# Local attention and whitening on one core: ScalarE's kept copies given out inside the halves of sums, some steps of the order moved, and one batch of writes issued from SyncE

## The chip, the cores and the metric

One core of a Trainium2 chip. The metric is the device time of one execution in microseconds (us); times stated for a kernel are the median of several executions. Engines are called PE (TensorE: matmuls and transposes; PEld is its weight load), DVE (VectorE), ACT (ScalarE), POOL (GpSimd) and SP (SyncE). SP, ACT and POOL also issue DMAs.

## What is computed

The input x has shape (4, 256, 64, 64), all in float32. Two layers follow one another; cut to what matters:

```python
# layer 0
k = conv(x, w1, 7x7, dilation 2, padding 6) + b1      # 256 -> 128 channels
k = conv(k, w2, 1x1) + b2                             # 128 -> 49
attn = softmax(k, axis=1)                             # one weight for each of 49 taps
shifts = stack([xp[:, :, 2*u:2*u+64, 2*v:2*v+64] for u in range(7) for v in range(7)])
y = einsum('bkchw,bkhw->bchw', shifts, attn)          # weighted sum of 49 shifted inputs
# layer 1, for each of 4 groups of 64 channels over all images
Sigma = eps*I + xc @ xc.T / m                         # xc: y less its mean
P = five Newton steps towards Sigma**(-1/2)
out = (P @ xc) * weight + bias
```

## The kernel before

**Convolution.** The two convolutions are merged into one with 49 outputs. By the dilation, each image falls into parities of rows and columns, and the 7x7 convolution is done on them as a transformed one (points of evaluation along rows, `ROWS` 0 to 5 and `INF`, and along columns, grouped in three `BANKS`). One step is `conv_step(k, i)` (line 828): the matmuls of one bank into a PSUM tile `cv` (L603) and their eviction by ACT into `pv` (L614, L619), in `conv_bank` (line 577); then `prepare` (line 819) makes the operands for the same bank of the next row: `weights` (DVE, and scalings on ACT at L481), `row_eval` (DVE; for row 0 two plain copies rb<-slot on ACT, L510) and `col_eval` (DVE into `xh`, and one plain copy xh<-rb on ACT, L545 or L551). For row 0 of an image `weights` also issues a load from SP, rb<-g0d, of weights kept in DRAM, and DMAs that copy pieces of them. `col_interp` and `row_interp` (DVE) bring results back to logits.

**Kept work of ACT.** The copies and scalings on ACT that `prepare` makes are not traced at once. They are put in the list `points`, and the next `conv_bank` traces them behind its own eviction; a dependency that orders issue only keeps them behind it. The list `later` does the same for the last copies of an interpolation (L710, L737), after bank 1 only.

**Attention.** Each image has four quarters, n = 4b to 4b+3. For a quarter, the softmaxed weights d are copied into a padded tile `zt` (`move_terms`, line 1095: eleven small copies, L1127 on ACT, or L1139 on DVE for the last image), written to a DRAM scratch `sd` by eight DMAs (L1146), and read back skewed as `band` and `bandz` by `load_band` (L1196, L1208, on SP). `weighted_sum` (L1316) then is a matmul of a block of transposed inputs with the band. A quarter is done in two halves:

- `first_half(n)` (line 1452): for each block, `make_blocks` transposes x on PE (L1252) and evicts it on ACT, xb<-tp (L1283) and for edges xbz<-tp (L1274); the sums; `store_y` evicts y in place of x (L1338, ACT). In between stand the turns of the quarter before: `turn_y` transposes y (L1388) and evicts yt<-tp (L1398, ACT); `moments` multiplies yt with itself into `sig` (L1407).
- `second_half(n, mid)` (line 1492): the same for the lower half, with the turns of its own upper half, `make_blocks` of the next quarter's first block, `moments`, and `bands(n + 1, last)`, which loads the next band and moves the terms of the quarter after it.
- `finish()` (line 1444) does the two turns and moments that the next first half would have done; for odd n it calls `move`, which spills a slot of x and y to DRAM (L1431) and loads the next image's x into it (L159), both from POOL.

**Order.** PE runs in the order of the trace, since every matmul is tied to the one before it. Evictions on ACT are marked with a high priority, and a scheduler that runs at compile time fixes each engine's order from priorities, dependencies and its own estimate of times. The main loop runs the convolution of image b and cuts it by cost into eight stretches; at the end of each, `gap(b, j)` runs what `plan` has put there, for instance the halves of sums of image b-1. With the steps' costs, the halves of image 0 stand in gaps (1,2) to (1,7), (2,0) and (2,1), with `finish` behind the fourth; those of image 1 one image later; those of image 2 in gaps (3,3) to (3,7), and its last three and all of image 3's behind the loop, where they are called by hand as `rest[...]`. The step in front of gap (2,0) and of gap (3,0) is `direct_inf`, a direct convolution of one row (L770).

Of the kernel before, what the change touches and what calls it, by code (L numbers as in the profile page):

```python
# [32 lines left out]
def kernel(  # L33
# [29 lines left out]
    nc = tc.nc  # L63
# [508 lines left out]

    slot = {}

    later, points = [], []

    def conv_bank(b, br, i, w):

        if i == 0:
            slot[b, br] = len(slot) % NV if b == 0 else (len(slot) - NV) % 2  # L580
        pts = BANKS[i]
        i0 = sum(len(k) for k in BANKS[:i])
        cv = cv_buf[ncv[0] % 2][:, : 3 * PT].rearrange("p (n q f) -> p n q f", n=3, q=Q9)
        ncv[0] += 1
        if b == 0:
            xv = {bc: xh[bc].rearrange("p (q e f) -> p e q f", e=2 * NCC, q=Q8) for bc in pts}
        else:
            xv = {
                bc: xh[bc].rearrange("p (e g q f) -> p e q g f", e=2 * NCC, g=2, q=Q8)
                for bc in pts  # L590
            }
        for k, bc in enumerate(pts):
            terms = [(sr, sc, cc) for sc in taps(bc) for sr in taps(br) for cc in range(NCC)]
            wv = w[bc].rearrange("p c (a r k) -> p c r a k", r=len(taps(br)), a=NCC)
            for j, (sr, sc, cc) in enumerate(terms):
                for h in range(2):
                    o = cv[
                        h * HB : h * HB + KT, k, sr : sr + Q8, 2 * sc : 2 * (sc + Q8)
                    ]
                    if b > 0:  # L600
                        o = o.rearrange("p q (g f) -> p q g f", g=2)
                    pe(
                        nc.tensor.matmul(  # L603
                            o,
                            wv[:, sc, sr, cc],
                            xv[bc][:, h * NCC + cc],
                            start=(j == 0),
                            stop=(j == len(terms) - 1),
                            skip_group_check=True,
                        )  # L610
                    )
        with tc.high_priority():
            full_ = len(pts) - (INF in pts)
            last = nc.scalar.copy(  # L614
                pv[:K2, slot[b, br], i0 : i0 + full_].rearrange("p n q b -> p (n q b)"),
                cv[:K2, :full_].rearrange("p n q f -> p (n q f)"),
            )
            if INF in pts:
                last = nc.scalar.copy(  # L619
                    pv[:K2, slot[b, br], i0 + full_].rearrange("p q b -> p (q b)").rearrange(  # L620
                        "p (q f) -> p q f", q=Q9
                    )[:, :, : 2 * Q8],
                    cv[:K2, full_, :, : 2 * Q8],
                )
        for waiting in (points, later) if i == 1 else (points,):
            while waiting:
                with tc.high_priority() if waiting is points else nullcontext():
                    copied = waiting.pop()()
                for one in copied if isinstance(copied, list) else [copied]:
                    tc.add_manual_dep(  # L630
                        one.ins,
                        last.ins.name,
                        mybir.DependencyInfo(
                            mybir.DependencyClass.NoSync, mybir.DependencyReason.DATA
                        ),
                        reason="later",
                    )

    def interpolate(pt, tmp, outs, cut, part=None, pairs=None):

# [187 lines left out]
    def conv_step(k, i):  # L828
        w = {bc: nxt.pop(bc) for bc in BANKS[i]}
        b, br = rows[k]  # L830
        conv_bank(b, br, i, w)
        end = b > 0 and br == ROWS[-1]
        if end:

            with in_order():
                if i == len(BANKS) - 2:
                    col_interp(b, br, 0)
                elif i == len(BANKS) - 1:
                    col_interp(b, br, 1)
                    row_interp(b, 1)  # L840
        last = i == len(BANKS) - 1 and br == ROWS[-2]
        if k + 1 < len(rows):
            with tc.high_priority() if last else nullcontext():
                prepare(k + 1, i, points.append)
        if i == len(BANKS) - 1 and not end:
            with in_order() if last else nullcontext():
                col_interp(b, br)
                if last:
                    row_interp(b, 0)
# [245 lines left out]
    def move_terms(n, after=None):  # L1095
# [46 lines left out]
        for g in range(CR):  # L1142
            for h in range(2):
                p0 = g * SW + h * TC
                queue = nc.sync if h and n == 4 * (B - 1) else nc.gpsimd
                dma = queue.dma_start(  # L1146
                    bass.AP(
                        tensor=D.tensor,
                        offset=D.offset + h * HS + g * RS,
                        ap=[[LS, TC], [CR * RS, NCH], [1, KS * WS]],  # L1150
                    ),
                    zt[p0 : p0 + TC, R : R + NCH * KS].rearrange(
                        "p (m e) w -> p m (e w)", e=KS
                    ),
                )
                if queue is nc.gpsimd:
                    written[:] = [dma]
# [283 lines left out]

    half_done = {-1}

    def finish():

        n = open_n.pop()
        for t8 in (2, 3):
            turn_y(n, t8)
        moments(n, 1)
        if n % 2:  # L1450
            move(n // 2)

    def first_half(n):
        last = open_n.pop() if open_n else None

        def turn(t8):
            if last is not None:
                turn_y(last, t8)

        def block(t8):  # L1460
            if (n, (t8, 0)) not in blocks:
                make_blocks(n, t8)

        block(0)
        turn(2)
        weighted_sum(n, 0, 0)
        block(1)
        weighted_sum(n, 0, 1)
        block(2)
        weighted_sum(n, 0, 2)  # L1470
        turn(3)
        weighted_sum(n, 0, 3)
        weighted_sum(n, 0, 4)
        move_terms(n + 1, store_y(n, 0))
        half_done.add(n)
        load_band(n + 1, 0)
        make_blocks(n, 3, y_dve.get((n, 0))) if (n, (3, 0)) not in blocks else None
        if last is not None:
            moments(last, 1)
            if last % 2:  # L1480
                move(last // 2)

    def bands(n, after=None):

# [4 lines left out]
            load_band(n, 1)  # L1489
            move_terms(n + 1, after)  # L1490

    def second_half(n, mid=None):
        turned = turn_y(n, 0)
        if n % 4 == 3:
            bands(n + 1, turned)
        weighted_sum(n, 1, 0)
        weighted_sum(n, 1, 1)
        turn_y(n, 1)
        weighted_sum(n, 1, 2)
        weighted_sum(n, 1, 3)  # L1500
        weighted_sum(n, 1, 4)
        if mid is not None:
            mid()
        last = store_y(n, 1)
        if n + 1 < 4 * B:
            make_blocks(n + 1, 0, y_dve.get((n, 1)))
        moments(n, 0)
        open_n.append(n)
        done.add(n)
        bands(n + 1, last)  # L1510

# [24 lines left out]
    for b in range(B):  # L1536
        hs = [
            (lambda *a, n=n, f=f: f(n, *a))
            for n in range(4 * b, 4 * b + 4)
            for f in (first_half, second_half)  # L1540
        ]
        if b + 2 < B:
            for j in range(8):
                plan(b + 1, 2 + j, hs[j])
                if j == 3:

                    plan(b + 1, 2 + j, finish)
        else:
            for j in range(8):
                if b == B - 1 or 3 + j >= NPC:  # L1550
                    rest.append(hs[j])
                else:
                    plan(b + 1, 3 + j, hs[j])
    for b in range(B - 1):
        for j in range(2) if b else ():
            plan(b + 1, b * j, lambda b=b, j=j: soft(b, j))

    slots[4] = store[4]
    pieces = read_x(halves(store[4]), 4, nc.sync)
    for j in range(2, 6):  # L1560
# [6 lines left out]
    for b in range(1, B):  # L1567
# [12 lines left out]
            steps.insert(0, (12, lambda b=b: direct_inf(b)))  # L1580
        j, at, whole = 0, 0, sum(c for c, _ in steps)
        for cost, f in steps:
            f()
            while rest_of:
                rest_of.pop()()
            at += cost
            if at * NPC >= (j + 1) * whole:
                gap(b, j)
                j += 1
    apool.release()  # L1590
    rpool = ctx.enter_context(tc.tile_pool(name="rp", bufs=1, reuse_waits="tile"))

# [29 lines left out]
    rest[1]()  # L1622
    move_terms(n + 1)
    rest[2]()
    finish()
    soft_start(1, False)
    move_terms(n + 2)
    for t8 in range(4):
        if (n, (t8, 0)) not in blocks:
            make_blocks(n, t8)  # L1630
    rest[3]()
    rest[4]()
    soft_rows(1, 1)
    for f in rest[5:-2]:
# [242 lines left out]
```

## Time and profile before

| what | value |
|---|---|
| times of 3 runs | 680.88, 682.57, 682.58 us; median 682.57 |
| profiled execution | 680.68 us; its span 678.7 us |
| PE busy | 648.2 us (96%) |
| PEld busy | 527.6 us (78%) |
| DVE busy | 566.3 us (83%) |
| ACT busy | 332.7 us (49%) |
| POOL busy | 117.2 us (17%) |
| granted TensorE clock | 0.996 |
| DMA moved | 126.09 MB |
| sd<-zt, POOL, 77 KB | 124 DMAs, 3.3 us from issue to landing in the median |
| spill<-slot, POOL, 2048 KB | 3 DMAs, 10.5 us |

The span runs from the first to the last instruction that the profile shows; the execution's own time has some 2 us around it. A matmul counts as busy from its start to an end that is modelled, so the busy share of PE says little; its idle time and who ended it say more. In a timeline row, the first two numbers are start and length in us, then come engine, line, operation, output<-input and shape, and in brackets the idle time before it and what ended that. The order of first blocks, turns and sums can be followed by line: L1252 transposes x, L1283 evicts it, L1316 sums, L1338 evicts y, L1388 turns it, L1398 evicts it, L1407 takes moments.

The gaps stand in the profile at these times (start of the first PE instruction of the half): gap (1,2) at 189.1, (1,5) with its `finish` at 238.7, (1,6) at 259.5, (2,0) at 289.5, (2,2) at 327.6, (2,5) at 379.6, (3,3) at 477.4. The last convolution ends at 540.8.

### The profile page before, as it was taken

To read this page: it belongs to the slowest core of one execution; us is meant where nothing else is said; L and a number is where in the kernel's file an instruction comes from. 1 tells how busy PE (TensorE), PEld (TensorE's weight loads), DVE (VectorE), ACT (ScalarE), POOL (GpSimd) and SP (SyncE) were. 2 spreads that over 40 slices of the span, in tenths; PEclk is the share of its full clock that TensorE was granted. 3 is DMA by queue.
4 is the path that set the end of the run, shared out by engine and by line. 5 is a ranking of instruction groups with operands and counts; after the bars stand their busy time and mean duration, and the time that the engine had idled before them with its cause. 6 is when DMAs were issued, how large, how long until landed. Compare 5 with 4: busy or idle time off the path is not lost.

```text
span 678.7 us, 19071 instructions
## 1 busy us (share of the span) xinstructions
PE 648.2 (96%) x7800; PEld 527.6 (78%) x7800; DVE 566.3 (83%) x1240; ACT 332.7 (49%) x862; POOL 117.2 (17%) x177
## 2 busy tenths in 40 slices
PE   6999999999999999999899999999999999999993
PEld 1439573357899988889899998999899999998430
DVE  3699999999389889999999589989998987633673
ACT  1424331023565555566755554464854566634663
POOL 0000550662213020001122020002130203400000
PEclk9999999999999999999999999999999999999998
DMA  8961899993599979313587485027374325649698
GB/s 318 248 162 67 138 262 361 217 185 50 116 208 224 228 160 370 120 60 84 166 269 245 139 279 189 2 67 190 94 199 111 71 63 123 166 98 384 237 404 354
DMA packets 110607, 126.09 MB, mean 186 GB/s; under 512 B 69255, under 2 KB 91896, under 8 KB 109368
## 3 DMA queue, kind: packets, MB, share of 16 engines
q1 hardware_dynamic: 93528, 69.03, 35.3%
q0 software_dynamic: 10944, 37.57, 22.1%
q10 hardware_dynamic: 6048, 18.27, 8.8%
q8 instruction: 61, 1.00, 0.6%
q14 instruction: 26, 0.21, 0.1%
HBM read 78.78 MB, written 52.36 MB: 193 GB/s over the span
## 4 chain that ended last, share of the span: by engine, by line
PE 67%; DVE 19%; ACT 6%; DMA 4%; issue 2%; POOL 0%; ACTq 0%; DVEq 0%; SPq 0%; POOLq 0%
PE cv L603 24%; PE y L1316 10%; PE cv L770 8%; PE acc L770 8%; PE sig L1407 4%; PE tp L1388 3%; DMA out_dram<-out 3%; PE tp L1252 2%; DVE pv L352 2%; DVE zz L352 2%; PE cv L251 2%; DVE xh L352 2%; DVE ct L352 2%; DVE zz L348 1%; DVE zz L345 1%
## 5 line engine op out<-in xcount | busy, mean ns | idle before, releaser
L603 PE MATMUL cv<-xh,wr 128*49 128x128 f32 x4160 | 232.6, 273 | 0.2
L603 PEld LDWEIGHTS cv<-xh,wr 128*49 128x49 f32 x4160 | 226.1, 124 | 3.3 <-issue 1.0
L1146 POOL DMA_DIRECT2D sd<-zt x124 | 65.2, 532 | 334.6 <-ACT zt L1127 269.6
L1316 PE MATMUL y<-band,xb 128*128 128x209 f32 x448 | 93.9, 342 | 4.7 <-ACT xb L1283 2.7
L1316 PEld LDWEIGHTS y<-band,xb 128*128 128x128 f32 x448 | 75.7, 190 | 6.0 <-ACT xb L1283 3.3
L614 ACT COPY pv<-cv 113x486 f32<-113x486 f32 (+2 forms) x60 | 26.0, 433 | 90.6 <-PE cv L603 90.3
L352 DVE SCALAR_TENSOR_TENSOR pv<-pv 113x162 f32<-113x162 f32 x176 | 53.1, 322 | 2.2 <-ACT pv L614 1.4
L1127 ACT COPY zt<-d 32x112 f32<-32x112 f32 (+2 forms) x132 | 38.5, 292 | 14.9 <-DVE d L997 9.3
L1398 ACT COPY yt<-tp 128x512 f32<-128x512 f32 x60 | 34.9, 593 | 21.1 <-PE tp L1388 20.5
L1388 PE MATMUL tp<-ident,slot 128*128 128x128 f32 x240 | 41.5, 296 | 1.0 <-ACT slot L1338 1.0
L1049 ACT ACTIVATE d<-tp,mx 128x49 f32<-128x49 f32 x96 | 27.5, 322 | 28.0 <-DVE mx L1046 28.0
L1252 PE MATMUL tp<-ident,slot 128*128 128x128 f32 x256 | 40.5, 282 | 0.0
L1407 PE MATMUL sig<-yt 128*64 128x65 f32 x1024 | 38.1, 225 | 2.3 <-ACT yt L1398 2.3
L1388 PEld LDWEIGHTS tp<-ident,slot 128*128 128x128 f32 x240 | 34.9, 205 | 6.1 <-issue 3.8
L1407 PEld LDWEIGHTS sig<-yt 128*64 128x64 f32 x1024 | 32.9, 137 | 8.2 <-ACT yt L1398 3.0
L1252 PEld LDWEIGHTS tp<-ident,slot 128*128 128x128 f32 x256 | 38.1, 204 | 0.2 <-issue 0.2
L1283 ACT COPY xb<-tp 128x512 f32<-128x512 f32 x52 | 30.5, 586 | 9.7 <-PE tp L1252 6.6
L352 DVE SCALAR_TENSOR_TENSOR xh<-ct 128x512 f32<-128x512 f32 x40 | 26.5, 692 | 10.2 <-PE cv L603 9.9
L770 PE MATMUL acc<-slot,tap 128*49 128x256 f32 (+7 forms) x224 | 34.7, 468 | 0.0
L770 PEld LDWEIGHTS acc<-slot,tap 128*49 128x49 f32 x224 | 16.0, 123 | 18.0 <-issue 15.5
L147 POOL DMA_DIRECT2D slot<-in_x_dram x12 | 20.4, 1700 | 53.8 <-DVE xh L352 38.2
L348 DVE TENSOR_TENSOR pv<-pv 113x162 f32<-113x162 f32 (+1 forms) x77 | 27.5, 366 | 0.3
(258 smaller groups left out, 1141.2 us busy)
## 6 DMA issues: line engine op xcount, KB each, us to landing
out_dram<-out SPq DMA_DIRECT2D x31, 512.0 KB, 5.9
band<-sd SPq DMA_DIRECT2D x64, 242.0 KB, 3.7
sd<-zt POOLq DMA_DIRECT2D x124, 77.0 KB, 3.3
wr<-gd ACTq DMA_DIRECT2D x14, 588.0 KB, 5.0
wr<-gd ACTq DMA_DIRECT2D x14, 490.0 KB, 4.8
slot<-in_x_dram POOLq DMA_DIRECT2D x12, 512.0 KB, 10.5
ahead<-in_x_dram POOLq DMA_DIRECT2D x12, 512.0 KB, 7.5
spill<-slot POOLq DMA_DIRECT2D x3, 2048.0 KB, 10.5
```

Of the source, the lines that this page charges most:

```text
L348: return in_turn(TT(o, a, b, ALU.subtract))
L352: return in_turn(STT(o, a, f, b, ALU.mult, ALU.add))
L603: nc.tensor.matmul(o, wv[:, sc, sr, cc], xv[bc][:, h * NCC + cc], start=(j == 0), stop=(j == len(terms) - 1), skip_group_check=True,)
L770: nc.tensor.matmul(ps[h * HB : h * HB + KT, :, o0:o1], w[v][:, cc], rhs, start=(j == 0 and k == 0), stop=(j == len(order) - 1), skip_group ...
L1127: ins = nc.scalar.copy(o, i)
L1146: dma = queue.dma_start(bass.AP(tensor=D.tensor, offset=D.offset + h * HS + g * RS, ap=[[LS, TC], [CR * RS, NCH], [1, KS * WS]],), zt[p0 : ...
L1252: nc.tensor.transpose(t[:, h * C + cc * P : h * C + (cc + 1) * P], tile_of(xt, cc, t8, h, pc), turned_by(n),)
L1283: (nc.vector.tensor_copy if n > 4 * B - 3 else nc.scalar.copy)(xb.rearrange("p a c -> p (a c)"), t[:, : 2 * C])
L1316: nc.tensor.matmul(y_ps[n, half, cc][:, q0 : q0 + nq, c0:c1], xb[:, cc * P : (cc + 1) * P], rhs, start=(k == 0), stop=(k == len(PIECES[hal ...
L1388: nc.tensor.transpose(t[:, h * C + cc * P : h * C + (cc + 1) * P], tile_of(yt, cc, t8, h, pc), turned_by(n),)
L1398: return nc.scalar.copy(yb.rearrange("p h a g c -> p (h a g) c")[:, :, :GW], t[:, : 2 * C].rearrange("p (e c) -> p e c", c=GW),)
L1407: nc.tensor.matmul(sig[g * GW : (g + 1) * GW, cc], yb[:, g, :GW], yb[:, g], start=(count[0] == 0), stop=end, skip_group_check=True,)
```

## The change

1. A list `held` and a flag `half_next`. The main loop sets the flag for a step that ends at a gap with a half in it (`half_gaps`). Then `conv_bank` does not give out `points` but moves them to `held`, and the half gives them out: a first half behind its second turn (or behind `store_y` where it has no turns), a second half behind its second turn.
2. Where such a step would prepare bank 0 of row 0 of the next image, `prepare` is called after the gap instead of before it.
3. `finish` for n = 1 and n = 5 runs inside `second_half`, behind its moments and ahead of `bands`; the moved terms then follow the last turn.
4. The `finish` behind `rest[2]` (n = 11) leaves its moments to the end of `rest[3]`, the first half of n = 12.
5. The first block of n = 0 is made in gap (1,1), one stretch earlier.
6. For n = 4, four of the eight writes of `move_terms` are issued from SP, as they already were for n = 12.

```diff
-    later, points = [], []
+    later, points, held = [], [], []
+    half_next, half_gaps, after_gap = [False], set(), []
...
-        for waiting in (points, later) if i == 1 else (points,):
-            while waiting:
...
+        if half_next[0]:
+            held.extend(points)
+            points.clear()
+        give_out(points, last)
+        if i == 1:
+            give_out(later, last)
+
+    def give_out(waiting, last):
+
+        while waiting:
+            with nullcontext() if waiting is later else tc.high_priority():
+                copied = waiting.pop()()
+            for one in copied if isinstance(copied, list) else [copied]:
+                tc.add_manual_dep(
+                    one.ins,
+                    last.ins.name,
...
         if k + 1 < len(rows):
-            with tc.high_priority() if last else nullcontext():
-                prepare(k + 1, i, points.append)
+            if half_next[0] and (i, rows[k + 1][1]) == (0, 0):
+                after_gap.append(lambda: prepare(k + 1, i, points.append))
+            else:
+                with tc.high_priority() if last else nullcontext():
+                    prepare(k + 1, i, points.append)
...
-                queue = nc.sync if h and n == 4 * (B - 1) else nc.gpsimd
+                queue = nc.sync if h and n in (4, 4 * (B - 1)) else nc.gpsimd
...
-    def finish():
+    def finish(late=None):
 
         n = open_n.pop()
         for t8 in (2, 3):
-            turn_y(n, t8)
-        moments(n, 1)
-        if n % 2:
-            move(n // 2)
-
-    def first_half(n):
+            turned = turn_y(n, t8)
+
+        def end():
+            moments(n, 1)
+            if n % 2:
+                move(n // 2)
+
+        end() if late is None else late.append(end)
+        return turned
+
+    def first_half(n, end=None):
...
-        turn(3)
+        turned = turn(3)
         weighted_sum(n, 0, 3)
         weighted_sum(n, 0, 4)
-        move_terms(n + 1, store_y(n, 0))
+        if turned is not None:
+            give_out(held, turned)
+        stored = store_y(n, 0)
+        give_out(held, stored)
+        move_terms(n + 1, stored)
...
+        if end is not None:
+            end()
...
-    def second_half(n, mid=None):
+    def second_half(n, mid=None, close=False):
...
-        turn_y(n, 1)
+        turned = turn_y(n, 1)
         weighted_sum(n, 1, 2)
         weighted_sum(n, 1, 3)
         weighted_sum(n, 1, 4)
+        give_out(held, turned)
...
         moments(n, 0)
         open_n.append(n)
+        if close:
+            last = finish()
         done.add(n)
         bands(n + 1, last)
...
-                plan(b + 1, 2 + j, hs[j])
-                if j == 3:
-
-                    plan(b + 1, 2 + j, finish)
+                half_gaps.add((b + 1 + (2 + j) // NPC, (2 + j) % NPC))
+                plan(b + 1, 2 + j, (lambda f=hs[j]: f(None, True)) if j == 3 else hs[j])
...
+                    half_gaps.add((b + 1, 3 + j))
                     plan(b + 1, 3 + j, hs[j])
...
+    plan(1, 1, lambda: make_blocks(0, 0))
...
+            half_next[0] = (at + cost) * NPC >= (j + 1) * whole and (b, j) in half_gaps
             f()
...
                 gap(b, j)
                 j += 1
+                while after_gap:
+                    after_gap.pop()()
...
-    finish()
+    ends = []
+    finish(ends)
...
-    rest[3]()
+    rest[3](ends.pop())
```

## The prediction, made before the changed kernel was run

> **What bounds the kernel now.** I read the page first, then TensorE's waits, then the timeline around each wait. TensorE (PE) is busy 96% of the span and idle 30.5 us; part of that is the start and the output at the end. So only idle time on PE itself can be won in between. Its list of waits (what waited and for whom; us in total, times, longest) names it:
>
> ```profile
> PE y L1316 <- ACT xb L1283: 2.7, 3, 1.1
> PE sig L1407 <- ACT yt L1398: 2.3, 4, 0.8
> PE y L1316 <- DMA band<-sd: 1.9, 2, 1.3
> PE y L1316 <- ACT xbz L1274: 1.4, 2, 1.1
> PE tp L1388 <- ACT slot L1338: 1.0, 3, 0.6
> ```
>
> Together 9.3 us, nearly all inside the halves of sums: ScalarE (ACT), only 49% busy, is at the wrong work for a microsecond. The timeline (start, length, instruction, idle before it and who ended it) shows two such places, the first half of n=0 and that of n=2:
>
> ```profile
> 189.75 0.68 ACT L545 COPY xh<-rb 128x512 f32<-128x512 f32 x1
> 190.31 0.61 ACT L1283 COPY xb<-tp 128x512 f32<-128x512 f32 x1
> 190.97 0.44 PE L1316 MATMUL y<-band,xb 128*128 128x209 f32 x1 [1.09 <-ACT xb L1283]
> ...
> 262.83 1.05 ACT L510 COPY rb<-slot 128x1024 f32<-128x1024 f32 x1 [0.30 <-issue]
> 263.88 0.74 ACT L1274 COPY xbz<-tp 64x256 f32<-64x256 f32 x2
> 264.68 0.57 PE L1316 MATMUL y<-bandz,xbz 128*128 128x96 f32 x3 [1.09 <-ACT xbz L1274]
> ```
>
> But PE is not the only limit. VectorE (DVE) waits for PE at 252.42 and then, by the stretches (columns PE, PEld, DVE, ACT, POOL), is full until 380:
>
> ```profile
> 252.42 0.64 DVE L352 SCALAR_TENSOR_TENSOR wr<-ct 128x196 f32<-128x196 f32 x2 [3.29 <-PE cv L603]
> ...
> 280.00:300.00 20.00, 19.22 (x206) 16.36 (x203) 20.00 (x47) 9.87 (x21) 0.00 (x0) 1.00 0.20 74
> 300.00:320.00 20.00, 20.00 (x294) 18.93 (x292) 19.93 (x38) 12.48 (x52) 0.22 (x1) 1.00 0.24 68
> ...
> 319.78 4.29 POOL L1146 DMA_DIRECT2D sd<-zt  x8 [55.60 <-ACT zt L1127]
> 325.48 1.60 SPq L1196 DMA_DIRECT2D band<-sd  x2
> ```
>
> That matters because the second image's attention weights come out of this full stretch: DVE's last shuffle of d ends at 315.20, zt copies, eight writes from 319.78, band loads at 325.48 and 326.71, and PE waits for them at 329.00 (0.65 us) and 331.75 (1.30 us). What PE wins between 252 and 329 it gives back there.
>
> **Part by part**, in PE idle time of this execution.
>
> First block. make_blocks(0,0) moves from 189.1 to the end of the direct convolution at 178.2: four transposes and one copy (0.61), the same number as before. x of slot 0 landed by 159.7, so they don't wait. The whole 1.09 goes; the bands of n=0 had landed by 187.6, so nothing is late behind it. The copy may delay the softmax exponentials of pc=1 by 0.6; cover is until their zt copies are written at 200.9. **1.09.**
>
> finish inside second_half, n=1 and n=5. At 245.5 the turns were ready, but five zt copies (1.50 us) stood before the yt copies. With the turns traced first, the yt copy starts at 245.48 and ends 0.6 later; PE, free at 245.95, waits 0.15 of the 0.82: 0.67 won. At 387.58 likewise 0.64 of 0.79. What moves behind: eleven zt copies (0.30 each) and their eight writes, at most 0.6 us later. They are of n=3 and n=7, whose bands SP loads at 265.39 and 403.41 and whose sums start at 290.1 and 429.3: covered. move(0) and move(2) are now traced before these writes, so the 2 MB spill (9.8 to 12.8 us) can go first on POOL's queue. The nearest row is n=6: the slot load issued at 357.86 between its first and second write made the later ones land near 370 and not near 361. Ten us late is still under the cover; without it each us would be PE's. In return the slot that direct_inf reads at 277.91 (landed 273.35) comes earlier. **0.67 and 0.64.**
>
> Prepared rows. row_eval's two rb copies (1.05 each) leave the half at 262.8; PE's 1.09 goes. The same edit stands before the third image, where PE had no wait: nothing.
>
> Held points. What is held is an xh copy (0.68 to 0.74) or scalings (0.52), now behind the half's turn copies. Only first halves with one gain: at 481.37, where ACT ran xh (0.74), yt, zz, xb, PE's 0.85 shrinks by 0.74. At 329 the band ends the wait, not ACT. At 293.38 (0.78) the step before is direct_inf, which holds nothing: no gain. The wait that is added is queue order: behind the held copies stand the evictions of y, for which PE waits only in the next half, over 10 us on; the copies' own readers are the next row's matmuls, over 3 us on. Cost 0; if a held copy slips before the last edge copy (PE waits 0.36 for one at 483.89), 0.74 in each of two first halves. **0.74.**
>
> Writes of n=4 on SP. The last write leaves POOL at 324.07. Four fewer there are 4 x 0.53 = 2.1 us of issue. The row that has this split is n=12: first write 562.94, band loads issued 568.56 and 569.48, that is 5.62 and 6.54 later, against 5.70 and 6.93 for n=4 on POOL alone. A rule speaks against the edit too: the Trainium skill (DMA: Bandwidth & Descriptors, Issuing engines are not separate DMA queues) says that spreading DMAs over engines saves only the sequencer's time, since all run on the same 16 DMA engines. By the rule alone the second load comes up to 2.1 earlier, by the row 0.4. Below nothing: SP issues nothing else from 292.3 to 325.4, so no loss. I take the row, **0.4**, and keep 2.1 for the range.
>
> finish at the end. 32 sig matmuls (1.17 us) move from 570.9 behind the first half of n=12. Their wait (0.25) goes, and they fill the idle 0.58 and 0.22 at 578.54 and 579.14, where PE waits for y's evictions. The last softmax's transposes start earlier, which its DVE chain (idle 1.22 before it) uses. yt isn't overwritten between, since that half turns nothing. **1.05.**
>
> **The sum.** Up to 252.4: 1.09 + 0.67 = 1.76, and DVE, released by PE there, moves by 1.76 too. PE's next 1.09 makes it early at 329, where the band comes only 1.76 + 0.1 earlier; at 331.75 the second band is 1.76 + 0.4 = 2.16 earlier while PE could be there at 328.6: it waits until 329.6. So 2.16 is what remains. Then DVE is idle again (7.46 before 390.55, PE released it) and gains add up: 0.64 + 0.74 + 1.05. **2.16 + 2.43 = 4.6 us.** The profiled execution took 680.68 (span 678.7), so 676.1; its time lies at the low end of the runs (680.88, 682.57, 682.58, median 682.57), from which it would be 678.0. I give the middle, **677.0**.
>
> **Rivals.**
> A, DVE does not hold PE back: the compile-time order of DVE or ACT changes with the new priorities, and the SP writes bring the rule's 2.1. Then 1.09, 0.78, 1.95 - 0.4 and 0.36 come on top of, in part instead of, the above: at most 8.4 us, 673.3. For it: waits sum to 9.3. Against: DVE's 20.00 of 20.
>
> B, the order shuffles the waits: held copies before the last edge copies (2 x 0.74), a zt copy before a yt elsewhere, the 0.64 lost. Net 0 to 2 us won: 679.5 to 681.5. For it: the order on ACT is fixed beforehand and PE's waits are all of that kind.
>
> C, slower: the load rb<-g0d. It belongs to the deferred preparation, so on SP it comes behind the half's band and edge loads. Before, it was issued at 256.78 and took 10.1 us; DVE first reads rb at 277.03, or 275.3 when 1.76 earlier. Behind the edge loads that end at 268.0 it leaves at 266.2, lands at 276.3 if it again takes 10.1: DVE waits 1.0. Behind the next half's edge loads, which wait for PE until 273.61 to 274.84, it lands at 283: DVE waits 8, in the full stretch, and the band of n=4 and PE with it. 676.1 + 8 = 684 by the profiled time. It decides from a landing after 275.3. Against: those edge loads are traced after it, and the spill that slowed it then comes earlier.
>
> That the change doesn't act is unlikely: the flag for a coming half is set from the same counts as the gap itself.
>
> **Chances.** Forecast (3 to 6.3 us won) 0.53; A 0.17; B 0.18, of which a third still beats 0.3%; C 0.12. 0.3% is 2.05 us, about what a measurement here can tell from no change: below 680.5 counts as faster. So faster 0.76, same 0.14, slower 0.10 (part of C ends within 0.3%). Range 673.5 to 681.0: from A's end to B's middle.
>
> **What would show it.** Right: no idle before the y at 190, before the sig after finish above 0.2, at 264; PE waiting for band near 327 and 329.5 on the new clock; DVE still full to 380; no wait for slot evictions near 575. Wrong: DVE idle between 252 and 315 for rb (C), new waits for xbz or xb (B), or no band wait and 3 us or more won by 332 (A).

## The result and the profile after

| kernel | profiled execution (span) | median of the runs | lowest to highest |
|---|---|---|---|
| before | 680.68 (678.7) us | 681.84 us, 4 runs | 680.88 to 682.58 |
| changed | 671.98 (670.2) us | 672.04 us, 4 runs | 671.95 to 672.60 |

The ratio of the changed kernel to the kernel before is 0.9859, with a 95% interval from 0.9842 to 0.9876. Between the two profiled executions lie 8.7 us, where the prediction had 4.6. Two of the four runs of the kernel before lie at 682.6: of its 49 runs beside the experiments, the 11 at 682.2 us or more have a mean granted clock of 0.991 or 0.992, and the other 38 (680.3 to 681.8) one of 0.994 to 0.996.

TensorE's waits in the changed kernel (what waited and for whom; us in total, times, longest), in the places of the list shown before:

```profile
PE y L1328 <- ACT xbz L1286: 1.1, 1, 1.1
...
PE sig L1419 <- ACT yt L1410: 0.9, 3, 0.4
...
PE y L1328 <- ACT xb L1295: 0.6, 1, 0.6
...
PE tp L1400 <- ACT slot L1350: 0.2, 1, 0.2
```

The line for the band, 1.9 us before, is gone; the prediction had it stay. The wait for xbz at the half of n=2, which was to go, is still there. The timeline of the changed kernel (columns as before) has it:

```profile
189.66 0.98 PE L1328 MATMUL y<-band,xb 128*128 128x209 f32 x4
...
261.02 1.04 ACT L510 COPY rb<-slot 128x1024 f32<-128x1024 f32 x1 [0.30 <-issue]
262.08 0.74 ACT L1286 COPY xbz<-tp 64x256 f32<-64x256 f32 x2
...
262.88 0.69 PE L1328 MATMUL y<-bandz,xbz 128*128 128x96 f32 x4 [1.11 <-ACT xbz L1286]
```

The first sum of n=0 no longer waits, but the row copy (L510) still stands between the edge copies (xbz) of n=2.

To see where the time went, each matmul of the sums and convolutions was paired with the same one of the kernel before, and the two start times subtracted. This **lead** of the changed kernel grows in steps:

| place (time in the kernel before) | predicted gain | growth of the lead | lead after it |
|---|---|---|---|
| first block, n=0 (179 to 191) | 1.09 | 1.31 | 1.31 |
| finish, n=1 (248) | 0.67 | 0.50 | 1.81 |
| row copies, n=2 (264) | 1.09, given back at 329 | 0.00 | 1.81 |
| first half of n=3 (293) | 0 | 0.20 | 2.01 |
| band of n=4 (329 to 332) | lead 2.16 after it | 2.37 | 4.38 |
| finish, n=5 (389) | 0.64 | 0.66 | 5.03 |
| 460 | 0 | 0.26 | 5.29 |
| held points (481 to 484) | 0.74 | 1.48 | 6.78 |
| 565 | 0 | 0.12 | 6.90 |
| finish at the end (575) | 1.05 | 1.63 | 8.53 |

Two things stand out: the band of n=4, and terms that came out larger than the idle time that the rows showed.

**At n=4** the view to read is ScalarE's timeline ahead of the band, with the issue of the writes and loads. Before:

```profile
315.26 0.86 ACT L1127 COPY zt<-d 128x56 f32<-128x56 f32 x3 [3.55 <-DVE d L997]
316.14 1.39 ACT L1338 ACTIVATE slot<-y,pivot_x 128x512 f32<-128x512 f32 x2
317.98 2.48 ACT L1127 COPY zt<-d 32x112 f32<-32x112 f32 x8
```

After:

```profile
310.85 1.36 ACT L1350 ACTIVATE slot<-y,pivot_x 128x512 f32<-128x512 f32 x2 [0.57 <-PE y L1328]
313.51 3.35 ACT L1139 COPY zt<-d 128x56 f32<-128x56 f32 x11 [0.85 <-issue]
...
316.19 2.10 POOL L1158 DMA_DIRECT2D sd<-zt  x4 [58.92 <-ACT zt L1139]
...
315.92 2.02 SPq L1158 DMA_DIRECT2D sd<-zt  x4
322.10 0.99 SPq L1208 DMA_DIRECT2D band<-sd  x2
```

VectorE did what the prediction says: its last shuffle of d ends at 313.42 in place of 315.19, 1.77 us earlier. But the first write leaves 3.86 us earlier (315.92 in place of 319.78). Before, ScalarE was in order at three of the eleven copies zt<-d, waited for d, and only then evicted y of n=3 and a block xb (1.8 us with the gap) before it did the other eight. After, these evictions stand ahead of all eleven and fall into the time in which ScalarE had waited 3.55 us for d. From the first write to the first band load it is 6.18 us, against 5.70 before: the second queue did not shorten that stretch.

### The profile page after: what moved, and what is told of

It reads as the page before. It is cut to its first block, busy times and chain, and to the rows that moved or that the text cites. A ratio compares the mean times of both kernels' runs of the same rounds, so it can differ in the third digit from the quotient of the medians.

```text
span 670.2 us, 19064 instructions
## 1 busy us (share of the span) xinstructions
PE 647.1 (97%) x7800; PEld 527.4 (79%) x7800; DVE 566.5 (85%) x1240; ACT 332.6 (50%) x862; POOL 115.0 (17%) x173
## 4 chain that ended last, share of the span: by engine, by line
PE 83%; DVE 10%; DMA 2%; ACT 2%; issue 1%; SPq 0%; POOL 0%; DVEq 0%; ACTq 0%; POOLq 0%
PE cv L604 30%; PE y L1328 13%; PE cv L779 10%; PE acc L779 9%; PE sig L1419 5%; PE tp L1400 4%; PE tp L1264 4%; PE cv L251 2%; DMA out_dram<-out 2%; PE tp L1730 2%; DVE zz L352 1%; DVE pv L352 1%; PE tp L1021 1%; DVE zz L348 1%; DVE ct L352 1%
## 5 line engine op out<-in xcount | busy, mean ns | idle before, releaser
L1158 POOL DMA_DIRECT2D sd<-zt x120 | 63.0, 532 | 295.0 <-ACT zt L1139 232.0
```

The lines of the kernel that those rows point to most:

```text
L1158: dma = queue.dma_start(bass.AP(tensor=D.tensor, offset=D.offset + h * HS + g * RS, ap=[[LS, TC], [CR * RS, NCH], [1, KS * WS]],), zt[p0 : ...
```

## The experiments

Two theories about n=4: the **order theory** (the compiler's order on ScalarE freed the band, and the second queue for the writes did next to nothing) and the **queue theory** (the second queue did it). About the sizes: a wait costs its **idle time** as shown, or the **start spacing** of the matmuls beyond what it is without a wait. The kernel before ran again beside the experiments, with medians of 680.97 (first four), 680.81 and 680.81 us. The changed kernel did not: its 672.04 is from the result's four runs, so differences from it of half a microsecond or less are not told apart. The edits are cut to what matters (`...`); `NoSync` in them stands for the dependency that orders issue only.

**b_close**, the kernel before with part 3 of the change alone (the lists of the other parts stay empty):

```diff
+        if close:
+            last = finish()
...
-                    plan(b + 1, 2 + j, finish)
+                plan(b + 1, 2 + j, (lambda f=hs[j]: f(None, True)) if j == 3 else hs[j])
```

> The kernel before with one part of the change: finish() is called inside second_half (after turn_y, before the bands) for the halves that had it as a step of their own; n = 4's writes stay on GpSimd's queue. Order theory (the compiler puts n = 4's copies of the moved terms in one run on ScalarE because of this part, and that alone brings n = 4's band early): the two finishes 0.50 and 0.66 us, the band of n = 4 about 1.9, sum 3.1 us faster than before, profiled at about 677.6; no wait for the band of n = 4 is left on TensorE. Queue theory (the second queue for n = 4's writes brought the band early): 1.2 us faster, profiled at 679.5; the two waits for the band (0.65 and 1.30 us) are still there.

Measured: 676.35 us, ratio to before 0.9923 (0.990 to 0.9946), profiled 676.46. Its zt copies stand in one run of eleven (314.69, 3.35 us), behind the evictions. One wait of 0.4 for the band is left. The lead over before grows by 1.84 at the band and by 0.57 and 0.55 at the two finishes, as the order theory has it; 0.92 more came at 293, 460 and 481, which the expectation lacked.

**b_sp4**, the kernel before with part 6 alone:

```diff
-                queue = nc.sync if h and n == 4 * (B - 1) else nc.gpsimd
+                queue = nc.sync if h and n in (4, 4 * (B - 1)) else nc.gpsimd
```

> The kernel before with one part of the change: the second half of n = 4's writes is issued by SyncE. Queue theory: the band of n = 4 lands about 2 us earlier, both waits for it go, 1.9 us faster than before, profiled at about 678.8. Order theory: no more than 0.2 us faster, profiled at 680.5 to 680.8, both waits still there.

Measured: 681.51 us, ratio 1.0009 (0.9997 to 1.002), profiled 680.67: nothing gained. TensorE in its timeline, beside 0.65 at 329.00 and 1.30 at 331.75 before:

```profile
329.38 0.98 PE L1316 MATMUL y<-band,xb 128*128 128x209 f32 x4 [1.01 <-DMA band<-sd]
330.93 0.97 PE L1316 MATMUL y<-band,xb 128*128 128x209 f32 x4
...
334.60 0.69 PE L1316 MATMUL y<-bandz,xbz 128*128 128x96 f32 x4 [0.34 <-ACT xbz L1274]
```

The second load is no longer late, but the wait for the first is longer by 0.36. Behind the second sum the lead over before is 0.8, and part 6 does save that much there. But the compiler also put one copy yt (333.59) ahead of the last edge copy xbz (334.19), TensorE waits for that at 334.60, and a lead of 0.2 is left. So the test is not of the queue alone. The queue theory, with 1.9 us and neither wait left, still fails here; the order theory was right on the time and wrong in that the second wait did go.

**a_pool4**, the changed kernel without part 6 (the same line, the other way round).

> The changed kernel with n = 4's writes all on GpSimd's queue again. Queue theory: slower than the changed kernel by 1.5 to 2 us (profiled at 673.5 to 674), with waits for the band of n = 4 back. Order theory: within 0.5 us of the changed kernel (profiled at 671.8 to 672.5), no wait for the band or one of at most 0.5 us.

Measured: 672.32 us, 0.28 above the changed kernel (profiled 0.39 above), no row of a band wait. So part 6 is worth 0.3 to 0.4 us at most, and the runs alone cannot tell it from nothing.

**a_split**, the changed kernel with n=4's order on ScalarE put back:

```diff
+        zts_of[n] = copies
...
                     last = nc.scalar.activation(o, i, AF.Identity, bias=shift[:, cc : cc + 1])
+                    if (n, half) == (3, 1):
+                        tc.add_manual_dep(last.ins, zts_of[4][2].ins.name, NoSync, reason="split")
```

> The changed kernel with ScalarE's two evictions of n = 3 and the copy behind them put back between the third and the fourth copy of n = 4's moved terms, as they stood before the change; nothing else differs. Order theory: first write of n = 4 some 1.8 us later, the wait for its band back on TensorE, 1.5 to 1.9 us slower than the changed kernel, profiled at about 673.7. Queue theory: the writes on two queues make up for it, no more than 0.4 us slower, profiled at 672.0 to 672.4.

Measured: 674.45 us, 2.4 above the changed kernel (profiled 2.2). The waits are back:

```profile
327.27 0.97 PE L1331 MATMUL y<-band,xb 128*128 128x209 f32 x4 [0.99 <-DMA band<-sd]
329.41 0.98 PE L1331 MATMUL y<-band,xb 128*128 128x209 f32 x4 [0.70 <-DMA band<-sd]
```

This kernel is also the test of the prediction's own step: with before's order kept, its lead over before is 2.34 behind the band. The prediction had 2.16.

**b_tie**, the reverse: the kernel before, with none of the change, and only the order at n=4 of the changed kernel. On every other engine its instructions stand as before.

```diff
-        if n % 4 == 3:
+        if n % 4 == 3 and n != 3:
             bands(n + 1, turned)
...
         last = store_y(n, 1)
+        if n == 3:
+            bands(n + 1, last)
```

> The kernel before with nothing of the change; only the first three copies of n = 4's moved terms stand behind the evictions of n = 3 and the copy after them on ScalarE, as in the changed kernel, in place of ahead of them. Order theory: both waits for the band of n = 4 go, 1.7 to 2.3 us faster than before, profiled at about 678.7. Queue theory (and any that needs another part of the change): no more than 0.3 us faster, both waits still there.

Measured: 678.70 us, ratio 0.9966 (0.9953 to 0.9979), profiled 678.70: 2.1 us faster than before.

```profile
312.81 1.36 ACT L1338 ACTIVATE slot<-y,pivot_x 128x512 f32<-128x512 f32 x2 [1.14 <-PE y L1316]
315.22 3.35 ACT L1127 COPY zt<-d 128x56 f32<-128x56 f32 x11 [0.59 <-issue]
...
329.67 0.98 PE L1316 MATMUL y<-band,xb 128*128 128x209 f32 x4 [0.18 <-DMA band<-sd]
```

The copies start where they started before (315.22 and 315.26), but all eleven in one run, and the writes leave at 317.91. Of the two waits, 0.18 us is left. This settles it: the order alone, in either kernel, is worth 2.1 to 2.4 us.

**a_rblate**, the row copies tied behind the half's last eviction:

```diff
-                nc.scalar.copy(r[2], xs[:, 0])
+                one = nc.scalar.copy(r[2], xs[:, 0])
+                if half_end:
+                    tc.add_manual_dep(one.ins, half_end[-1].ins.name, NoSync, reason="half_end")
...
         stored = store_y(n, 0)
+        half_end.append(stored)
```

> The changed kernel with the prepared rows' copies rb<-slot tied behind the half's last eviction, which takes the wait for xbz (1.11 us idle, 1.25 by start spacing) out of the half of n = 2; but the compiler then puts n = 4's copies of the moved terms in the order of before again. Order theory: gains 1.25 and loses 2.2, so 0.9 us slower than the changed kernel, profiled at about 672.9, waits for the band of n = 4 back. Queue theory: 1.2 us faster, profiled at 670.8.

Measured: 675.89 us (673.74 to 678.02), 3.9 above the changed kernel: both theories missed. The wait at 262.88 went (lead 1.26), was given back at 291, 1.95 more was lost at 330, not to the band, and another 1.7 just behind it, where TensorE's clock was reduced (last section):

```profile
329.24 0.33 ACTq L417 DMA_DIRECT2D wr<-gd  x1
329.61 0.59 ACT L1302 COPY xb<-tp 128x512 f32<-128x512 f32 x1 [2.46 <-DMA wr<-gd]
```

A DMA that ScalarE itself issues stood in its order until 329.24, and the block xb behind it waited with it. So this run says nothing on the two theories.

**a_rbtie**, the same with n=4's order tied as in b_tie.

> The same as a_rblate, with n = 4's copies of the moved terms tied behind the evictions of n = 3 as in the changed kernel. Order theory: 1.25 us faster than the changed kernel by start spacing (1.1 by the idle time shown), profiled at about 670.7; no wait for the band of n = 4. If the rows' copies come late for the convolution that reads them, less than that, and a wait for xh in the following piece.

Measured: 674.23 us, 2.2 above the changed kernel, where 1.25 below was expected. The lead of 1.25 from 262.88 is gone at 291.35, where TensorE now waits 1.91 for xb, and 1.57 us more are lost behind that. ScalarE's timeline:

```profile
288.30 0.72 ACT L753 ACTIVATE lgx<-lgx,bias 113x512 f32<-113x512 f32 x1 [2.71 <-DVE lgx L352]
288.92 0.57 ACT L798 COPY zz<-cv 113x512 f32<-113x512 f32 x1
...
290.72 0.58 ACT L1302 COPY xb<-tp 128x512 f32<-128x512 f32 x1
```

The lgx waits for VectorE until 288.30, in the changed kernel until 288.31. So VectorE had not moved, and what TensorE had won it gave back here, 40 us earlier than the prediction said for this stretch. But xb also stands behind two scalings (L481) in ScalarE's order; the next run moves those.

**a_rbmul**: a_rbtie with the two scalings wr<-wr in front of that xb tied behind it.

```diff
+            muls_of[br, i] = muls
...
+            if (n, t8) == (3, 1):
+                for one in muls_of[0, 1]:
+                    tc.add_manual_dep(one.ins, made_xb.ins.name, NoSync, reason="muls")
```

> a_rbtie with two scalings wr<-wr of the next convolution's weights tied behind the block xb that TensorE waits for at 289.4 to 291.35. If it is ScalarE's in-order list behind the lgx that waits for VectorE that gave the 1.25 us back there: xb about 0.9 us earlier, TensorE's wait 1.0 us in place of 1.9, no reduced clock behind it (1.57 us in a_rbtie), so 0.9 us faster than the changed kernel, profiled at about 671.1. If VectorE sets the end of this stretch whatever the order: no faster than the changed kernel, profiled at 672.0.

Measured: 671.88 us (671.49 to 672.35), 2.35 below a_rbtie, but only 0.16 below the changed kernel, which is no difference that these runs can tell. At 291 the wait is 1.09 as expected and 0.86 was won back there, and the 1.57 behind it too. So of the 1.25 given back in a_rbtie, 0.86 lay in the place of two scalings in ScalarE's order; some 0.4 is still given back, behind the lgx that waits for VectorE. Little of it lasts: of its lead over the changed kernel of 0.6 us at 329, 0.3 is left at the end.

**best3**: a_rbmul with the turns between the moments in the two finishes:

```diff
         if close:
-            last = finish()
+            for t8 in (2, 3):
+                moments(n, 0, (2 * t8 - 4, 2 * t8 - 3))
+                last = turn_y(n, t8)
+            moments(n, 1)
+            move(n // 2)
```

> a_rbmul, and in the two finishes that now lie inside second_half each turn of y is put ahead of two moments that are ready, so that the waits for yt (0.38 us each at 244 and 382) are filled: 0.4 us each by the idle time, 0.5 by start spacing, so 0.8 to 1.0 us faster than a_rbmul and 1.7 to 1.9 us faster than the changed kernel, profiled at about 670.2.

Measured: 672.40 us, 0.5 slower than a_rbmul, not 0.8 to 1.0 faster. The waits for yt at both places are gone from the list, yet from the first of these matmuls to the following convolution it takes 3.90 us at n=1 (242.37 to 246.27) against 3.57 (242.17 to 245.74). The alternation costs more than the wait it fills; why is open.

**a_nolate**, the changed kernel without part 4 (`finish(ends)` is again `finish()`).

> The changed kernel with the last finish's moments back at the finish's own place. Priced by the start spacing of the matmuls: 1.5 us slower than the changed kernel, profiled at about 673.5. Priced by the idle time that the rows of before show (0.25, 0.58 and 0.22): 1.05 us slower, profiled at about 673.0.

Measured: 673.45 us, 1.41 above the changed kernel (profiled 1.28), nearer to the 1.5 of start spacing than to the 1.05 of idle time. The rows show why idle time is too little. Without part 4:

```profile
570.21 0.58 PE L1328 MATMUL y<-bandz,xbz 128*128 128x96 f32 x4
571.37 0.39 PE L1400 MATMUL tp<-ident,slot 128*128 128x128 f32 x1 [0.59 <-ACT slot L1350]
571.97 0.63 PE L1400 MATMUL tp<-ident,slot 128*128 128x128 f32 x3 [0.21 <-ACT slot L1350]
572.43 0.36 PE L1328 MATMUL y<-bandz,xbz 128*128 128x96 f32 x2
```

In the changed kernel:

```profile
568.85 0.58 PE L1328 MATMUL y<-bandz,xbz 128*128 128x96 f32 x4
569.36 1.15 PE L1419 MATMUL sig<-yt 128*64 128x65 f32 x32
570.44 0.83 PE L1400 MATMUL tp<-ident,slot 128*128 128x128 f32 x4
571.10 0.58 PE L1328 MATMUL y<-bandz,xbz 128*128 128x96 f32 x4
```

From the first of these rows to the last it is 2.22 us without the moments and 2.25 with them. 0.80 us of shown idle time took in 1.08 us of work.

**a_nofirst**, the changed kernel without part 5 (the `plan(1, 1, ...)` line removed).

> The changed kernel without the step that makes the first block of x ahead of its half. Priced by start spacing: 1.35 us slower than the changed kernel, profiled at about 673.3. Priced by the idle time in the row of before (the prediction's step): 1.09 us slower, profiled at about 673.1.

Measured: 673.19 us, 1.15 above the changed kernel; between the two prices, so it doesn't decide. Its profiled execution (677.91) holds a single wait of 5.2 us elsewhere, for which the other five (672.86 to 673.52) are too short, so only the median is used.

**a_noheld**, the changed kernel without part 1:

```diff
-        if half_next[0]:
-            held.extend(points)
-            points.clear()
```

> The changed kernel without the held points: what the convolution before a half prepares stays ahead of the half's turns on ScalarE. Priced by start spacing: 1.5 us slower (0.96 and 0.52 at 481 to 484), profiled at about 673.5. The prediction's step: 0.74 us slower, profiled at about 672.7. The copies of n = 4's moved terms keep their place in either case, so no wait for its band comes back.

Measured: 674.08 us, 2.04 above the changed kernel (profiled 2.12). In the traces 0.63 and 0.52 are lost at 477 to 479, and 0.18 and 0.51 at the first half of n=4:

```profile
331.28 0.69 PE L1325 MATMUL y<-bandz,xbz 128*128 128x96 f32 x4 [0.34 <-ACT xbz L1283]
...
476.59 0.98 PE L1325 MATMUL y<-band,xb 128*128 128x209 f32 x4 [0.45 <-ACT xb L1292]
...
479.10 0.69 PE L1325 MATMUL y<-bandz,xbz 128*128 128x96 f32 x4 [0.35 <-ACT xbz L1283]
```

So part 1 also pays at n=4, once the band no longer hides what it saves there. Neither expectation had that. The later wait at both places, the one for xbz, comes from a change of order, as ScalarE's rows of a_noheld show:

```profile
474.62 0.74 ACT L545 COPY xh<-rb 128x512 f32<-128x512 f32 x1
...
476.56 1.14 ACT L1283 COPY xbz<-tp 64x256 f32<-64x256 f32 x3
478.08 0.59 ACT L1407 COPY yt<-tp 128x512 f32<-128x512 f32 x1 [0.38 <-PE tp L1397]
478.69 0.36 ACT L1283 COPY xbz<-tp 64x256 f32<-64x256 f32 x1
```

In the changed kernel:

```profile
475.08 1.51 ACT L1286 COPY xbz<-tp 64x256 f32<-64x256 f32 x4
476.62 0.59 ACT L1295 COPY xb<-tp 128x512 f32<-128x512 f32 x1
477.10 0.59 ACT L1410 COPY yt<-tp 128x512 f32<-128x512 f32 x1
477.58 0.68 ACT L545 COPY xh<-rb 128x512 f32<-128x512 f32 x1
```

Without the held points a copy yt, which itself waits for TensorE, stands ahead of the last edge copy; with them it stands behind all four. The same happens at n=4.

No kernel of these beats the changed one by more than the runs can tell apart.

## Why the prediction was wrong

**Forecast: 677.0, range 673.5 to 681.0; measured 672.04, faster than the range.** The direction was right; three things made it too small. The sum of gains was 4.6 and the profiled executions lie 8.7 apart: of the 4.1 missing, 2.2 are at the band of n=4 and 1.7 behind it.

**The band of n=4, "it waits until 329.6. So 2.16 is what remains": this is the step that failed.** It carried VectorE's 1.77 us through to the writes as if the copies between them kept their order. The shuffle moved by 1.77, and with the old order the lead behind the band is 2.34 (a_split), so the step holds for what it considered. What it did not ask was which of ScalarE's instructions stand between d and the first write. There were two evictions and one block, and they moved ahead: 2.1 us with nothing else changed (b_tie), 2.4 when undone (a_split). So TensorE did not wait for the band, kept what it had won, and its lead behind the band is 4.38. Of the two kernels with one part of the change, the one with finish inside second_half (b_close) has the new order; why the compiler chose it there was not shown. The choice is fragile: in a_rblate a tie on two row copies 50 us earlier brought the old order back.

**The held points at 0.74 and the last finish at 1.05 were mis-sized.** The held copy stood ahead of the wait at 481.37, and the prediction took the copy's length off it. The wait at 483.89 is not in its sum (rival A alone counted it). That wait came from the copy yt ahead of the last edge copy, and went with the change of order that the held points brought. Both went, 1.48 in the traces, and 2.04 with n=4 (a_noheld). The last finish brought 1.63 in the lead and 1.41 when undone (a_nolate). Both terms were summed from idle time, which starts at a matmul's modelled end, and the next matmul does not wait for that: at 479.90 the transposes last 0.63 by the row, but in the unhindered pairs the sum starts 0.47 after them, so the 0.85 shown at 481.37 was 1.00 of lost time.

**The base.** The profiled sum gave 676.1, and 0.9 was added for the median of three runs, two of which lay at 682.6. The medians of the kernel before beside the experiments were 680.81 to 680.97, so the profiled 680.68 was the better base.

**What held.** First block 1.09 (1.31 in the lead, 1.15 when undone); the finishes 0.67 and 0.64 (0.50 and 0.66). The writes of n=4 at 0.4 are 0.3 (a_pool4) or nothing in the end (b_sp4, where 0.8 was won at the band and mostly lost right behind it). The row of n=12 and the rule of the Trainium skill (DMA: Bandwidth & Descriptors, Issuing engines are not separate DMA queues) both stood against more: four fewer issues on POOL, 2.1 us of sequencer time, left the way from the first write to the band load at 6.18 us. The load leaves right behind the landing of a write (325.43 and 325.48 before, 321.97 and 322.10 after), not behind its issue.

**The row copies, 1.09, won nothing, but for another reason than given.** The prediction had both of them in the half of n=2. Before, only one stood there (262.83; the other at 278.25), and that one stayed (261.02). b_close, which lacks part 2, has both copies at the same places of ScalarE's order (262.23 and 266.28) as the changed kernel (261.02 and 265.49). So calling `prepare` later did not move them; tying them did (a_rblate). No kernel with part 2 alone was run. When the copies are really moved, the gain is given back at 291 (a_rbtie), 0.86 us of it to ScalarE's order and only some 0.4 to VectorE's pace (a_rbmul), and hardly any of it reaches the end. So the reading of the full stretch was right in part.

**The rivals.** A came nearest in time (673.3), and its sign came: no band wait, and 4.38 us won by 332. Its half about the compile-time order was right. Its other terms were not: the row copies brought nothing in place of 1.09, and the writes on SP 0.3 in place of up to 2.1. That its total lies so near is in part luck. B's new waits for xb and xbz did not come. C's did not either: the load rb<-g0d kept its place in SyncE's order, ahead of the band loads, and landed at 269.57, before the 275.3 from which it would have cost time. What it costs behind the half was not tested.

## What to carry to other kernels

Follow a chain instruction by instruction through each in-order engine: between the producer's end and the first dependent DMA, list what else stands in that queue, and ask whether the change can reorder it, since an order fixed at compile time can flip on an edit elsewhere; if a good order appears by chance, tie it down. Price a wait by the start spacing of matmuls against an unhindered pair, not by the idle time in the row. When one wait is predicted to remain, count also what other parts would be worth if it went.

## What the hardware showed that was not expected

**A single wait of under 2 us can be followed by a reduced TensorE clock.** In a_rbtie, by stretches (columns PE, PEld, DVE, ACT, POOL, then the granted clock), behind the wait of 1.91 us:

```profile
288.00:291.00 3.00, 1.44 (x11) 1.25 (x9) 3.00 (x9) 2.70 (x6) 0.00 (x0) 1.00 0.23 91
291.00:293.00 2.00, 1.65 (x5) 1.49 (x6) 2.00 (x7) 1.92 (x6) 0.00 (x0) 0.61 0.61 251
293.00:295.00 2.00, 2.00 (x10) 1.96 (x9) 2.00 (x5) 1.02 (x2) 0.00 (x0) 0.54 0.00 0
295.00:297.00 2.00, 2.00 (x41) 1.87 (x40) 1.80 (x3) 1.62 (x3) 0.00 (x0) 1.00 0.00 0
```

For some 4 us the clock is near half, each matmul of the sums falls 0.17 us further behind its pair, and 1.57 us are lost, nearly as much as the wait itself. In a_rblate it is the same behind a wait of 1.79 (0.50 from 332 to 334).

The length of the wait does not decide it alone. The same execution of a_rblate also has the wait at 291, as long as in a_rbtie, and there the clock stayed at 1.00:

```profile
291.13 0.97 PE L1335 MATMUL y<-band,xb 128*128 128x209 f32 x4 [1.92 <-ACT xb L1302]
...
291.00:293.00 2.00, 1.87 (x12) 1.87 (x13) 2.00 (x6) 1.92 (x6) 0.00 (x0) 1.00 0.61 251
```

It also stayed at 1.00 behind the 1.30 us of the kernel before at 331.75 and behind 1.09 in a_rbmul, in their profiled executions. Executions of one kernel differ too: the mean granted clock of a_rblate was 0.995 in its run of 673.74 us and 0.992 in the profiled one of 675.69; by estimate, 4 us at half clock out of 674 make just 0.003. The Trainium skill (TensorE: Matmul & The Clock Gate, Part 1: The HAM clock gate) has a half-rate state after an idle window of about 3.4 us; here a wait of little over half of that was enough at times. What decides was not measured.
